# A graph transformer of two layers: layer 1's second weights in seven products too, token sums and shifts moved to GpSimd, the end of each normalization moved to ScalarE

## The chip, the core and the metric

The kernel runs on one core of a Trainium2 chip. The core has five engines, each with an instruction queue of its own that it takes strictly in order: TensorE (PE in the profile), VectorE (DVE), ScalarE (ACT), GpSimd (POOL) and SyncE (SP, which only issues transfers). They wait for each other by semaphores. The metric is the time of the whole program on the device in microseconds, the median over runs.

## The reference

2708 tokens of 512 values go through two layers of the same form. `adj` is a sparse 0/1 matrix, and a token attends only to its neighbours.

```python
q = (h @ Wq.T + bq).reshape(n, 8, 64)      # k, v likewise
scores = where(mask == 0, -1e9, q.k / 8);  attn = softmax(scores)
attn_out = (attn @ v) @ Wo.T + bo
h1 = _layer_norm(h + attn_out, ln1_g, ln1_b)
ff = relu(h1 @ W1.T + b1) @ W2.T + b2      # 512 -> 2048 -> 512
h2 = _layer_norm(h1 + ff, ln2_g, ln2_b)
```

The normalization is `(x - mu) * rsqrt(var + 1e-5) * g + b`. Everything is f32.

## The kernel before, in words

The tokens are sorted by their number of neighbours into 22 groups of 128 (the last has 20), and the groups are taken in 11 blocks of two. Attention goes by lists: for every token GpSimd fetches the key and value rows of its neighbours by gathers (L1113, two neighbours for each of 128 tokens to a chunk). VectorE multiplies and sums them (L1150, L1156, L1182, L1189), and ScalarE takes exponentials and scales the values (L1169, L1176).

The order of all queues is written by hand: each engine gets its instructions in the order in which the Python code records them. For each block the main loop runs over 16 hidden chunks, f = 0 to 15. At each f it records the hidden product on TensorE (`pf`, four products of 128x256) and its relu on ScalarE (`ft`). At some f it records a step of the next block: the `attended` steps at f = 10 to 12 (turned context, output projection `o`, first normalization into `h`), `turned` at f = 15, and as many attention chunks as a table of paces allows (`advance`). So the attention of the next block runs beside the feed-forward of this one.

The feed-forward's second product comes in two forms. In `feed_forward` each hidden chunk meets its half of W2 in two products of 512 columns. In `feed_forward_by_seven`, used in layer 0 for blocks 2 to 9, two hidden chunks and two halves of tokens and of columns are seen as 2x2 matrices, and multiplied by seven products of 128x256 in place of eight, in Winograd's manner. Three more matrices made of W2 (`form`) are fetched for every pair of chunks from `form_d`; four sums of the hidden chunks (`sums`, 128x128 each) are made for each of seven pairs; the eighth pair goes the ordinary way. The results lie in four banks of PSUM, `a0`, `a1`, `c0`, `c1`, and are put together by one copy on ScalarE and eight additions on VectorE. The four banks leave two for hidden products (`ps_f`) where the ordinary form has three.

`norm` (L1265) is the layer normalization: statistics, `mv` and `va` on VectorE, `rd` (a power of -1/2 of one column) on GpSimd, then two passes of VectorE over the 128x512 tile, of which the first subtracts the mean and applies the gain, and the second (L1281) applies `rd` and adds the shift. The shift is `ln1_b + b2` after the first normalization, and `ln2_b` (in layer 0 with the next layer's `bo`) after the second. Since the tile holds more than the product needs, `flip` takes the surplus away while a turned tile is copied out of PSUM (`nb2`, `nbo`, the negated vectors as columns).

In layer 0 the finished `z` tiles are turned and multiplied into the next layer's keys and values during the next block (`keys_values`, f = 5 to 8). In layer 1 they are written to the output by a scatter of GpSimd (`put`).

Of the kernel before, what the change touches and what calls it, by code (L numbers as in the profile page):

```python
# [18 lines left out]
P = 128  # L19
# [35 lines left out]
PACE7 = (0.0,) * 4 + (0.6,) + (1.3,) * 4 + (0.6,) * 2 + (0.0,) * 2 + (0.5, 0.8, 2.4)  # L55
FORMED = 1
FORMS = (3, 5, 7, 9, 11, 13, 15)
# [426 lines left out]
def by_edges(ctx: ExitStack, tc: tile.TileContext, x, xT, adj, layers, out, redo):  # L484
# [71 lines left out]
    form_d = dram.tile([NFC // 2 - 1, 3, P, 2 * P], F32, name="form_d")  # L556
# [81 lines left out]
    def raw_columns(w, names, place):  # L638

        cols = []  # L640
        for i, name in enumerate(names):
# [3 lines left out]
            cols.append((t, raw, 1.0 if name == "bv" else -1.0))  # L645
# [619 lines left out]
    def norm(z, r, gain, shift, st=None, between=None):  # L1265
# [7 lines left out]
        nc.vector.tensor_scalar(va[:r], mv[:r, 1:2], EPS, None, ALU.add)  # L1273
# [7 lines left out]
        nc.vector.scalar_tensor_tensor(z[:r], z[:r], rd[:r], shift[:r], ALU.mult, ALU.add)  # L1281
# [20 lines left out]
    class Layer:  # L1302
# [5 lines left out]
        def load_first(self):  # L1308
# [7 lines left out]
            self.unsettled = raw_columns(w, ("bv", "b2"), place)  # L1316
            self.bv, self.nb2 = [col[0] for col in self.unsettled]
# [15 lines left out]
        def settle(self):  # L1333
            for t in self.unsettled:
                if len(t) == 2:
                    nc.vector.tensor_tensor(t[0], t[0], t[1], ALU.add)
                    continue
                to, raw, sign = t
                pr = ps.tile([P, DM], F32, tag="g", name="pr")
                nc.tensor.transpose(pr[:, :NC], raw, ident[:NC, :NC])  # L1340
                nc.vector.tensor_scalar(to, pr[:, :NC], sign, None, ALU.mult)
            self.unsettled = []
# [20 lines left out]
        def load_next(self):  # L1363
# [4 lines left out]
            self.unsettled += raw_columns(nxt, ("bo",), place)  # L1368
            self.nbo = self.unsettled[-1][0]
# [64 lines left out]
        def attended(self, block, got, xbs=None):  # L1434
# [16 lines left out]
            for i, xb in enumerate(xbs):  # L1451
# [7 lines left out]
                norm(h, r, self.g1, self.e1b2)  # L1459
# [6 lines left out]
        def turned(self, block, hs):  # L1466
            hT = dn.tile([P, NC, 2 * P], F32, tag="hT", name="hT", bufs=1)
            c0 = 0
            for g, h in zip(block, hs):
                r = size(g)  # L1470
                flip(h, r, hT[:, :, c0 : c0 + r], self.nb2)
                c0 += r
            return hT

        def feed_forward(self, block, hs, hT):
# [77 lines left out]
            for g, a, h in zip(block, accs, hs):  # L1553
# [15 lines left out]
                norm(z, r, self.g2, self.e2, st)  # L1569
                if self.n == NL - 1:  # L1570
                    put(out, ident_i[:r, g : g + 1], z[:r], "out")
# [15 lines left out]
        def form(self, j):  # L1587
# [3 lines left out]
            t2, t3, t4 = self.slots if j < NFC // 2 - 2 else self.other_slots  # L1591
# [4 lines left out]
            for i, t in enumerate((t2, t3, t4)):  # L1596
                nc.sync.dma_start(out=form_d[j, i], in_=t)
# [7 lines left out]
        def ask_forms(self, upto):  # L1605

            while self.asked < upto:
                n = self.asked
                j, i = n // 3 % (NFC // 2 - 1), (2, 0, 1)[n % 3]
                nc.sync.dma_start(out=self.slots[i], in_=form_d[j, i])  # L1610
# [471 lines left out]
```

## Time and profile before

| | |
|---|---|
| median of 3 runs | 1830.28 us (1830.05 to 1832.14) |
| span of the profiled execution | 1827.1 us |
| busy: TensorE, VectorE, ScalarE, GpSimd | 1807.5, 1457.5, 949.1, 798.9 us |
| a block of layer 0 in seven products | 75.5 to 76.5 us |
| a block of layer 1 | 63.7 us |

The profile is one execution. A row of time has the start, the length, the engine, the line, the operation, output and inputs, shapes, and in brackets how long the engine was idle before it and what ended that. A row of a group has the count, the busy time, the mean of one in nanoseconds, and the idle time before them. An f32 product appears as two records. Names are those of the program: `kv` a chunk of key and value rows, `pf` a hidden product in PSUM, `ft` and `forms` its relu in SBUF, `h` a tile of the residual stream (also the finished z), `u` the helper tiles of the seven products.

### The profile page before, as it was taken

Reading aid. Unit: us, or ns where it says so; the run is one execution under the profiler, and the core shown is the slowest. Engines: PE = TensorE matmul, PEld = TensorE weight load, DVE = VectorE, ACT = ScalarE, POOL = GpSimd, SP = SyncE. Lnnn points to the kernel's source line nnn. Section 1 sums busy time; section 2 is a strip of 40 time slices with the busy share of each in tenths; the row PEclk is TensorE's granted clock in tenths of the full one; section 3 lists DMA queues with packets and bytes.
Section 4 is the critical chain, followed back from the end, with each engine's and each line's share of the span. In section 5 each row is a group of like instructions: output and inputs, shape, how many; then the busy total and the mean of one; then the engine's idle time right before and its main releaser. Section 6 shows DMA issues by size and latency. Waiting matters only on the chain.

```text
span 1827.1 us, 22528 instructions
## 1 busy us (share of the span) xinstructions
PE 1807.5 (99%) x6563; PEld 1162.6 (64%) x6563; DVE 1457.5 (80%) x2447; ACT 949.1 (52%) x3271; POOL 798.9 (44%) x745
## 2 busy tenths in 40 slices
PE   9999999999999999999999999999999999999998
PEld 4444456666777867778677644666666666666666
DVE  5887778988989889898895257887898888889853
ACT  5771435645556545564543213665665565567531
POOL 3334755534455544454430042353464555456302
PEclk9999999999999999999999999999999999999999
DMA  9997987757576676765652876745564664555300
GB/s 340 369 335 256 371 283 245 236 169 241 195 255 228 197 236 196 219 233 181 228 191 70 287 257 248 285 160 180 178 228 150 228 224 169 195 197 194 133 14 21
DMA packets 158061, 393.80 MB, mean 216 GB/s; under 512 B 17514, under 2 KB 60894, under 8 KB 157928
## 3 DMA queue, kind: packets, MB, share of 16 engines
q0 software_dynamic: 70608, 252.12, 40.2%
q1 hardware_dynamic: 77162, 118.55, 18.7%
q10 hardware_dynamic: 10158, 21.61, 3.1%
q8 instruction: 53, 0.87, 0.2%
q14 instruction: 80, 0.66, 0.1%
HBM read 338.78 MB, written 53.44 MB: 215 GB/s over the span
## 4 chain that ended last, share of the span: by engine, by line
PE 89%; DVE 5%; issue 2%; ACT 2%; DMA 1%; POOL 1%; POOLq 0%; SPq 0%; DVEq 0%
PE pf L1523 18%; PE a L1496 17%; PE pf L1653 9%; PE k L620 8%; PE v L620 8%; PE q L620 8%; PE o L620 8%; PE c L1643 4%; PE a L1643 3%; PE tp L1293 2%; DVE sc L1156 1%; DVE kv L1150 1%; DMA forms<-form_d 1%; PE a L1677 1%; PE a L1673 1%
## 5 line engine op out<-in xcount | busy, mean ns | idle before, releaser
L1113 POOL DMA_INDIRECT kv<-kv_d,listed x420 | 524.0, 1248 | 291.2 <-DVE acc L1189 133.9
L1523 PE MATMUL pf<-hT,w 128*128 128x256 f32 (+1 forms) x1792 | 393.2, 367 | 0.1
L1523 PEld LDWEIGHTS pf<-hT,w 128*128 128x128 f32 x1792 | 323.5, 190 | 103.1 <-issue 64.4
L1496 PE MATMUL a<-w,ft 128*128 128x512 f32 x800 | 373.1, 592 | 0.0
L1176 ACT ACTIVATE kv<-kv,p 128x64 f32<-128x64 f32 x1232 | 311.0, 335 | 5.0
L1275 POOL TENSOR_TENSOR rd<-va,mhalf 128x1 f32<-128x1 f32 (+1 forms) x88 | 80.5, 914 | 520.6 <-DVE va L1273 520.5
L1150 DVE TENSOR_TENSOR kv<-kv,q 128x1024 f32<-128x1024 f32 (+1 forms) x222 | 256.9, 1157 | 13.3 <-DMA q<-q_d,ident_i 10.9
L1156 DVE TENSOR_REDUCE sc<-kv 128x16 f32<-128x1024 f32 (+1 forms) x222 | 257.9, 1162 | 7.6
L1189 DVE TENSOR_TENSOR acc<-acc,kv 128x1024 f32<-128x1024 f32 (+2 forms) x178 | 205.4, 1154 | 37.6 <-ACT kv L1176 23.0
L1653 PE MATMUL pf<-hT,w 128*128 128x256 f32 x1024 | 233.1, 379 | 1.6 <-ACT ft L1664 1.6
L1496 PEld LDWEIGHTS a<-w,ft 128*128 128x128 f32 x800 | 150.1, 190 | 113.2 <-issue 101.3
L1653 PEld LDWEIGHTS pf<-hT,w 128*128 128x128 f32 x1024 | 193.9, 190 | 35.4 <-issue 7.9
L1534 ACT ACTIVATE ft<-pf,b 128x256 f32<-128x256 f32 (+1 forms) x208 | 95.0, 459 | 197.6 <-PE pf L1523 195.2
L1169 ACT ACTIVATE p<-sc,listed 128x8 f32<-128x8 f32 x420 | 104.0, 296 | 147.2 <-DVE sc L1156 135.7
L620 PE MATMUL o<-wo,cT 128*128 128x512 f32 x336 | 151.0, 593 | 1.0 <-ACT cT L1298 1.0
L1664 ACT ACTIVATE ft<-pf,b 128x256 f32<-128x256 f32 x96 | 44.9, 468 | 160.5 <-PE pf L1653 160.5
L1182 DVE TENSOR_TENSOR kv<-kv,p 128x512 f32<-128x512 f32 (+1 forms) x178 | 123.4, 693 | 4.5 <-ACT p L1169 4.3
L620 PEld LDWEIGHTS o<-wo,cT 128*128 128x128 f32 x336 | 63.4, 190 | 74.7 <-issue 65.5
L745 DVE MAX8 tops<-code 128x8 f32<-128x247 f32 (+2 forms) x242 | 78.6, 400 | 28.3 <-ACT code L740 28.3
L1281 DVE SCALAR_TENSOR_TENSOR h<-h,rd,ln_b 128x512 f32<-128x512 f32 (+1 forms) x88 | 65.9, 749 | 39.5 <-POOL rd L1275 39.5
L1220 ACT ACTIVATE cx<-acc,su 128x64 f32<-128x64 f32 (+1 forms) x352 | 88.2, 333 | 12.9 <-DVE su L1212 7.4
L1455 DVE TENSOR_TENSOR h<-o,xb 128x512 f32<-128x512 f32 (+1 forms) x44 | 30.3, 688 | 80.0 <-PE o L620 65.0
(232 smaller groups left out, 2323.5 us busy)
## 6 DMA issues: line engine op xcount, KB each, us to landing
aj<-in_adj SPq DMA_DIRECT2D x42, 677.0 KB, 6.3
forms<-form_d SPq DMA_DIRECT2D x168, 128.0 KB, 4.2
kv_d<-kvs ACTq DMA_DIRECT2D x21, 512.0 KB, 5.5
xg<-in_xT SPq DMA_DIRECT2D x19, 512.0 KB, 7.4
w<-in_W SPq DMA_DIRECT2D x16, 512.0 KB, 6.2
kv<-kv_d,listed POOLq DMA_INDIRECT x420, 6.3
zT_d<-zT SPq DMA_DIRECT2D x22, 256.0 KB, 5.1
xb_d<-h SPq DMA_DIRECT2D x21, 256.0 KB, 5.7
```

Source lines behind the costliest of these rows:

```text
L620: nc.tensor.matmul(o[:r], xs(c), wm[:, c, :], start=(c == 0), stop=(c == NC - 1))
L1113: return nc.gpsimd.indirect_dma_start(out=to, out_offset=None, in_=table[:, :], in_offset=bass.IndirectOffsetOnAxis(ap=s, axis=0), bounds_ ...
L1150: nc.vector.tensor_tensor(kv[:r, :c, :DM], kv[:r, :c, :DM], self.q[:r].unsqueeze(1).to_broadcast([r, c, DM]), ALU.mult,)
L1156: nc.vector.tensor_reduce(self.sc[:r, s0 : s0 + c, :], kv[:r, :c, :DM].rearrange("p s (h d) -> p s h d", d=DK), AX.X, ALU.add,)
L1169: nc.scalar.activation(p[:r, s, :], self.sc[:r, s, :], AF.Exp, bias=minus[:r, g, s : s + 1])
L1176: nc.scalar.activation(to[:, i, hd], kv[:r, i, DM + h * DK : DM + (h + 1) * DK], AF.Copy, scale=p[:r, s0 + i, h : h + 1],)
L1182: nc.vector.tensor_tensor(to[:, 0, :].rearrange("p (h d) -> p h d", d=DK), kv[:r, 0, DM:].rearrange("p (h d) -> p h d", d=DK), p[:r, s0, : ...
L1189: nc.vector.tensor_tensor(self.acc[:r, :c, :], self.acc[:r, :c, :], kv[:r, :c, DM:], ALU.add)
L1496: nc.tensor.matmul(a[:r, cols], fts[f][:, c0 : c0 + r], self.w2[f // 2][:, f % 2, cols], start=(f == 0), stop=(f == NFC - 1),)
L1523: nc.tensor.matmul(pf[:, :w], self.w1[f // 2][:, c, f % 2 * P : f % 2 * P + P], hT[:, c, :w], start=(c == 0), stop=(c == NC - 1),)
L1643: nc.tensor.matmul(to, left, right, start=start, stop=stop)
L1653: nc.tensor.matmul(pf[:, :W], self.w1[j][:, c, f % 2 * P : f % 2 * P + P], hT[:, c, :], start=(c == 0), stop=(c == NC - 1),)
```

## The change

Layer 1 takes the seven products in blocks 0 to 9 (`FIRST7`), with a pace table and a `form_d` of its own. Its three extra matrices are formed in the last block of layer 0 and during the first queries of layer 1, in three places of the gathers' ring (`staged`). All four late query projections of layer 1 are done ahead of its first block, since the place of Wq then holds the fetched forms.

The token sums go from VectorE to GpSimd. In `norm`, `va` goes to GpSimd, and the second pass becomes a scaling on ScalarE without a shift; the shift is added by GpSimd (`shifted`) when the tile has been turned, or, in layer 1, before it is scattered. The columns that `flip` applies now add `ln1_b`, `ln2_b`. Only the two groups of the very last block keep the old second pass.

```diff
+FIRST7 = (FORMED + 1, 0)
...
-    def norm(z, r, gain, shift, st=None, between=None):
+    def norm(z, r, gain, st=None, between=None, shift=None):
...
-        nc.vector.tensor_scalar(va[:r], mv[:r, 1:2], EPS, None, ALU.add)
+        nc.gpsimd.tensor_scalar(va[:r], mv[:r, 1:2], EPS, None, ALU.add)
         rd = small.tile([P, 1], F32, tag="rd", name="rd")
         nc.gpsimd.tensor_tensor(rd[:r], va[:r], mhalf[:r], ALU.pow)
...
         if between:
             between()
-        nc.vector.scalar_tensor_tensor(z[:r], z[:r], rd[:r], shift[:r], ALU.mult, ALU.add)
+        if shift is not None:
+            nc.vector.scalar_tensor_tensor(z[:r], z[:r], rd[:r], shift[:r], ALU.mult, ALU.add)
+            return
+        nc.scalar.activation(z[:r], z[:r], AF.Copy, scale=rd[:r])
+
+    def shifted(z, r, shift):
+        nc.gpsimd.tensor_tensor(z[:r], z[:r], shift[:r], ALU.add)
...
-                norm(h, r, self.g1, self.e1b2)
+                norm(h, r, self.g1)
...
-                flip(h, r, hT[:, :, c0 : c0 + r], self.nb2)
+                flip(h, r, hT[:, :, c0 : c0 + r], self.e1)
                 c0 += r
+            for g, h in zip(block, hs):
+                shifted(h, size(g), self.e1b2)
...
-                norm(z, r, self.g2, self.e2, st)
+                norm(z, r, self.g2, st, shift=self.e2 if apart else None)
...
+        def staged(self):
+
+            slots = []
+            for _ in range(3):
+                place = at.tile([P, SLOTS, 2 * DM], F32, tag="kv", name="forms", bufs=KVB)
...
-                nc.vector.tensor_tensor(s[:, 0], f1[:, P:], f0[:, P:], ALU.add)
...
+                nc.gpsimd.tensor_tensor(s[:, 0], f1[:, P:], f0[:, P:], ALU.add)
+                nc.gpsimd.tensor_tensor(f0[:, P:], f0[:, :P], f0[:, P:], ALU.subtract)
+                nc.gpsimd.tensor_tensor(s[:, 1], s[:, 0], f0[:, :P], ALU.subtract)
+                nc.gpsimd.tensor_tensor(s[:, 2], f1[:, :P], s[:, 1], ALU.subtract)
...
-            norm(zA, P, self.g2, self.e2, between=lambda: stB.append(spread(zB)))
-            norm(zB, P, self.g2, self.e2, stB[0])
+            norm(zA, P, self.g2, between=lambda: stB.append(spread(zB)))
+            norm(zB, P, self.g2, stB[0])
+            if self.n == NL - 1:
+                for g, z in zip(block, hs):
+                    shifted(z, P, self.e2)
+                    put(out, ident_i[:, g : g + 1], z, "out")
...
-                flip(z, r, zT[:, :, :r], self.nbo)
+                flip(z, r, zT[:, :, :r], self.e2c)
                 zTs.append(zT)
+                shifted(z, r, self.e2)
...
-            seven = n == 0 and FORMED < k < NB - 1
+            seven = FIRST7[n] <= k < NB - 1
...
+                    if f > 6 and f % 2:
+                        nxt.form((f - 7) // 2, staged[(f - 7) // 2])
```

How the queues change is seen in three places. The first is ScalarE's queue at the end of a seven block of layer 0; `u` is the copy that begins the putting together, L1664 the next block's relus. Before:

```order
L1176 ACTIVATE acc<-kv,p 128x64 x8
L1695 COPY u_5593<-c_4991 128x256
L1664 ACTIVATE ft<-pf,b_1157 128x256 x4
L1664 ACTIVATE forms<-pf,b_1157 128x256
L1169 ACTIVATE p<-sc,listed 128x8 x2
```

With the change (L1686 are the relus, L1288 the new scaling):

```order
L1180 ACTIVATE acc<-kv,p 128x64 x8
L1717 COPY u_5618<-c_5012 128x256
L1288 ACTIVATE h<-h,rd 128x512 x2
L1686 ACTIVATE ft<-pf,b_1158 128x256 x4
L1686 ACTIVATE forms<-pf,b_1158 128x256
L1173 ACTIVATE p<-sc,listed 128x8 x2
```

Two scalings that read `rd` now stand between the copy of `u` and the next block's relus.

The second is ScalarE's queue around the output projections, f = 10 to 15 of the same block; `cT` is the turned context that a projection reads. Before:

```order
L1298 ACTIVATE cT<-tp,bv 128x128 x4
L1169 ACTIVATE p<-sc,listed 128x8 x2
L1176 ACTIVATE kv<-kv,p 128x64 x8
L1664 ACTIVATE forms<-pf,b_1157 128x256
L1298 ACTIVATE cT<-tp,bv 128x128 x4
L1664 ACTIVATE ft<-pf,b_1157 128x256 x3
```

With the change:

```order
L1308 ACTIVATE cT<-tp,bv 128x128 x4
L1173 ACTIVATE p<-sc,listed 128x8 x2
L1180 ACTIVATE kv<-kv,p 128x64 x8
L1686 ACTIVATE forms<-pf,b_1158 128x256
L1288 ACTIVATE h<-h,rd 128x512
L1308 ACTIVATE cT<-tp,bv 128x128 x4
L1686 ACTIVATE ft<-pf,b_1158 128x256
L1288 ACTIVATE h<-h,rd 128x512
L1686 ACTIVATE ft<-pf,b_1158 128x256 x2
```

The first scaling stands ahead of the second `cT`, the second ahead of the relu of f = 13.

The third is GpSimd's queue at the end of a block of layer 1. Before:

```order
L1275 TENSOR_TENSOR rd<-va,mhalf 128x1
L1076 DMA out<-h,ident_i 2708x512
L1275 TENSOR_TENSOR rd<-va,mhalf 128x1
L1076 DMA out<-h,ident_i 2708x512
L1113 DMA kv<-kv_d_112,listed 128x1024 x14
```

With the change (L1277 is `va`, L1291 a shift, L1647 to L1650 the sums of one pair):

```order
L1277 TENSOR_SCALAR va<-mv 128x1
L1279 TENSOR_TENSOR rd<-va,mhalf 128x1
L1291 TENSOR_TENSOR h<-h,ln_b 128x512
L1080 DMA out<-h,ident_i 2708x512
L1291 TENSOR_TENSOR h<-h,ln_b 128x512
L1080 DMA out<-h,ident_i 2708x512
L1647 TENSOR_TENSOR forms<-ft 128x128
L1648 TENSOR_TENSOR ft<-ft 128x128
L1649 TENSOR_TENSOR forms<-forms,ft 128x128
L1650 TENSOR_TENSOR forms<-ft,forms 128x128
```

Shifts and the next block's sums stand in the queue that held gathers and scatters, and the sums come behind both scatters.

More of the change, by code (lines that the diff above doesn't have):

```diff
@@ L555, in by_edges @@
     xb_d = [None] + [dram.tile([N, DM], F32, name=f"xb_d{n}") for n in range(1, NL)]
-    form_d = dram.tile([NFC // 2 - 1, 3, P, 2 * P], F32, name="form_d")
+    form_d = [dram.tile([NFC // 2 - 1, 3, P, 2 * P], F32, name=f"form_d{n}") for n in range(NL)]
     rec_d = dram.tile([P * NT, 2 * LIST], F32, name="rec_d")
@@ L1912, in by_edges @@
                 next(early[n])
-            streamed = now.queries(order[18 : 2 * AHEAD])
+            streamed = now.queries(order[18:])
             next(streamed)
             now.query(order[17], both[:, 1])
-            advance(0.6)
-            next(streamed)
-            advance(0.6)
+            for _ in order[18:21]:
+                advance(0.6)
+                next(streamed)
             *_, hs = early[n]
             early[n] = hs, now.turned(blocks[0], hs)
-            asking = now.queries(blocks[AHEAD])
-            next(asking)
             finish(streamed)
@@ L1925, in by_edges @@
             now.load_w2(NFC // 2 - 1)
+            now.prepared()
         hs, hT = early[n]
@@ L1960, in by_edges @@
                 if more and f == NFC - 1:
-                    finish(asking)
                     hT = now.turned(blocks[k + 1], hs_next)
-                advance((PACE7 if seven else (PACE if k else PACES)[n])[f])
-                if f in (0, 3, 7, 9) and (f or k):
-                    next(asking, None)
+                advance((PACE7[n] if seven else (PACE if k else PACES)[n])[f])
                 if k == 0 and len(now.w1) < NFC // 2 and f % 2 == 0:
```

52 lines of the change are left out of this document (27 added, 25 removed).

## The prediction

> **What bounds the kernel now.** I read the page first, then the stretches, then the order of time at the ends of blocks.
>
> ```profile
> PE 1807.5 (99%) x6563; PEld 1162.6 (64%) x6563; DVE 1457.5 (80%) x2447; ACT 949.1 (52%) x3271; POOL 798.9 (44%) x745
> ```
>
> Stretches (columns: length, then busy PE, PEld, DVE, ACT, POOL with counts, clock, DMA share, GB/s): one block of layer 0 in seven products, the turn to layer 1, one block of layer 1.
>
> ```profile
> 592.36:668.86 76.50, 75.71 (x311) 56.79 (x311) 67.44 (x114) 43.05 (x164) 37.74 (x30) 1.00 0.67 218
> 1003.00:1058.00 55.00, 54.36 (x251) 31.80 (x250) 16.15 (x33) 9.63 (x27) 4.78 (x5) 1.00 0.82 275
> 1403.40:1467.10 63.70, 63.70 (x226) 41.11 (x225) 55.20 (x72) 39.59 (x149) 33.27 (x28) 1.00 0.56 207
> ```
>
> TensorE sets the time: it has no gap in layer 1 and 0.79 us of gaps in 76.5 in layer 0. So work taken from the others is worth nothing, work taken from TensorE is worth its full time, and any wait put in front of TensorE costs its full time.
>
> **Fewer products.** Two stretches of the chain of waits (start, length, records):
>
> ```profile
> 547.15 10.36 PE pf L1653 x48
> 1398.27 5.15 PE a L1496 x12
> ```
>
> A product is two records. One 512 columns wide takes 2 x 5.15/12 = 0.858 us, one 256 wide 2 x 10.36/48 = 0.432. A layer 1 block had 32 wide ones in its second product: 27.5 us. In seven it has 49 narrow ones (21.2), and for the last pair 2 wide and 4 narrow (3.4): 24.6. The gain is 2.9 us in each of 10 blocks: **-28.8 us**.
>
> **The closing pass on ScalarE.** This step decides. ScalarE now ends each normalization, and takes its queue in order. Its rows at the end of a seven block read: copy u, scale zA, scale zB, then the relus of the next block. The scale of zB needs rd of zB, which needs statistics over the whole finished block. The next block's first hidden product needs no z, but its relu now stands behind that scale. Seven blocks have two places for hidden products, so the third waits for the first one's relu. This is how such a wait looks today, once for 0.79 us:
>
> ```profile
> 666.87 1.99 PE L1653 MATMUL pf<-hT,w 128*128 128x256 f32 x8 [0.79 <-ACT ft L1664]
> ```
>
> The end of a layer 0 block, in order of time:
>
> ```profile
> 622.38 0.59 PE L1643 MATMUL a<-w,forms 128*128 128x256 f32 x2
> 622.81 10.52 PE L1653 MATMUL pf<-hT,w 128*128 128x256 f32 x48
> 624.12 0.37 DVE L1696 TENSOR_TENSOR h<-u,h 128x256 f32<-128x256 f32 x1
> 624.74 0.47 ACT L1664 ACTIVATE ft<-pf,b 128x256 f32<-128x256 f32 x1 [2.65 <-PE pf L1653]
> 628.20 0.68 DVE L1269 BATCH_NORM_STATS2 st<-h 128x6 f32<-128x512 f32 x1
> 629.44 0.93 POOL L1275 TENSOR_TENSOR rd<-va,mhalf 128x1 f32<-128x1 f32 x1 [6.20 <-DVE va L1273]
> 630.46 0.73 DVE L1281 SCALAR_TENSOR_TENSOR h<-h,rd,ln_b 128x512 f32<-128x512 f32 x1
> 631.62 0.93 POOL L1275 TENSOR_TENSOR rd<-va,mhalf 128x1 f32<-128x1 f32 x1 [1.25 <-DVE va L1273]
> ```
>
> The next block starts at 622.81; its first relu follows at 624.74, at once. rd of zB ends at 632.55, 9.7 us after the start. VectorE came late to this chain: its first addition starts 1.3 us after the block's end. The same place with VectorE idle before:
>
> ```profile
> 1003.27 0.42 DVE L1696 TENSOR_TENSOR h<-u,h 128x256 f32<-128x256 f32 x1 [12.19 <-ACT u L1695]
> 1003.91 4.19 PE L1523 MATMUL pf<-hT,w 128*128 128x148 f32 x32
> 1009.67 0.73 DVE L1281 SCALAR_TENSOR_TENSOR h<-h,rd,ln_b 128x512 f32<-128x512 f32 x1
> 1010.83 0.92 POOL L1275 TENSOR_TENSOR rd<-va,mhalf 128x1 f32<-128x1 f32 x1 [1.27 <-DVE va L1273]
> ```
>
> Here rd of zB ends at 1011.75, 7.8 us after the start. In the changed kernel zA's closing pass is gone from between (0.7 us less), and va moves to GpSimd for about what it took on VectorE. That leaves 7.2 to 9.1 us. Then come the scale (nearest row: a ScalarE copy of that shape) and the first relu:
>
> ```profile
> L1737 ACT COPY kvs<-v 128x512 f32<-128x512 f32 x21 | 12.3, 586 | 106.0 <-PE v L620 106.0
> L1664 ACT ACTIVATE ft<-pf,b 128x256 f32<-128x256 f32 x96 | 44.9, 468 | 160.5 <-PE pf L1653 160.5
> ```
>
> So the first relu ends 8.2 to 10.1 us after the block's start, while TensorE wants the third product's place after two (2 x 1.73 = 3.45 us). It stands still for 4.8 to 6.7 us. I take 6.0, nearer the late row, since most blocks are crowded like it. Nothing can cover it: only hidden products stand there in TensorE's queue. Eight blocks of layer 0 and ten of layer 1 end so: 18 x 6.0 = **+108 us** (86 to 121). Late next: everything tied to the next hidden products.
>
> **The same pass in the middle of a block.** The scale of the first h tile now stands ahead of the copy-out of the second cT, which the second o product needs.
>
> ```profile
> 592.19 3.60 PE L620 MATMUL o<-wo,cT 128*128 128x512 f32 x8
> 596.26 1.14 ACT L1298 ACTIVATE cT<-tp,bv 128x128 f32<-128x128 f32 x4 [1.11 <-PE tp L1293]
> 597.97 0.68 DVE L1455 TENSOR_TENSOR h<-o,xb 128x512 f32<-128x512 f32 x1
> 600.66 0.93 POOL L1275 TENSOR_TENSOR rd<-va,mhalf 128x1 f32<-128x1 f32 x1 [0.42 <-DVE va L1273]
> 600.82 3.60 PE L620 MATMUL o<-wo,cT 128*128 128x512 f32 x8
> ```
>
> With these times rd ends at 601.59, the scale at 602.2, the copy-out at 603.3, and the second o starts 2.5 us late. But VectorE took up the first o 2.3 us after it ended; without that lateness the loss is 0.2. The token sums that leave VectorE give part of it back. I take 1.2 in the eight blocks of layer 0, where a bias is added too, and nothing in layer 1: **+10 us** (0 to 20, or 45 if layer 1 pays too).
>
> **Sums and shifts on GpSimd.** 28 sums of 128x128 and four shifts of 128x512 a block; nearest rows: GpSimd's integer sum of 128x128 and its 128x512 sum below.
>
> ```profile
> L734 POOL TENSOR_TENSOR aj<-aj,diag 128x128 int32<-128x128 int32 x20 | 8.7, 433 | 29.6 <-DMA aj<-in_adj 29.6
> 148.07 0.17 DVE L803 TENSOR_TENSOR run<-run 128x22 f32<-128x22 f32 x1
> 148.28 1.29 POOL L958 TENSOR_TENSOR kvs<-kvs,bk 128x512 f32<-128x512 f32 x1 [2.43 <-issue]
> 148.36 1.25 DVE L803 TENSOR_TENSOR run<-run 128x20 f32<-128x20 f32 x1
> ```
>
> That is 28 x 0.43 + 4 x 1.29 = 17.3 us of GpSimd a block. The last row matters: a VectorE sum of two SBUF tiles, 0.17 us by itself, took 1.25 and ended with the GpSimd sum beside it. The two exclude each other. VectorE loses the sums and four closing passes a block, and gets these waits instead. While TensorE pauses 6 us a block, I count both moves as nothing (layer 1's own adds for the seven products too); if GpSimd becomes the bound it is rival 1. The Trainium skill, "SBUF — State Buffer", section "Who interferes with whom", says the same: a VectorE instruction with two SBUF inputs and a GpSimd instruction that reads SBUF block each other for the whole instruction. The trace agrees (1.25 for 0.17).
>
> **TensorE's clock after a pause.** The only long pause in the trace is the program's end:
>
> ```profile
> 1818.00:1819.00 1.00, 0.24 (x2) 0.00 (x0) 0.69 (x2) 0.00 (x0) 0.00 (x0) 1.00 0.09 16
> 1823.00:1824.00 1.00, 0.00 (x0) 0.00 (x0) 0.00 (x0) 0.00 (x0) 0.00 (x0) 0.79 0.62 238
> 1824.00:1825.00 1.00, 0.00 (x0) 0.00 (x0) 0.00 (x0) 0.00 (x0) 0.00 (x0) 0.50 0.13 41
> ```
>
> The last product ends at 1818.24, and the granted clock falls to half at about 1823.6, 5.3 us later. My pauses of 4.8 to 6.7 us lie on both sides of that. How long half speed lasts shows at the program's start:
>
> ```profile
> 1.59 3.36 PE L540 MATMUL pr<-ones 128*128 128x128 f32 x14 [1.59 <-POOL ones L537]
> 612.45 1.04 PE L1293 MATMUL tp<-ident,h 128*128 128x128 f32 x8
> ```
>
> The warm-up products took 0.24 us each for 3.4 us, later ones of that size 0.13 or less. If a pause costs as much, 1.7 us is lost; with half of 18 pauses affected: **+15 us** (0 to 31). The Trainium skill, "TensorE: Matmul & The Clock Gate", Part 1, puts the gate on free-running windows of about 3.4 us; by it nearly every pause of 6 us would cost this, and the term would be near its upper end.
>
> **The turn between layers.** Forming layer 1's second weights is 28 subtractions:
>
> ```profile
> L1595 DVE TENSOR_TENSOR forms<-w,forms 128x256 f32<-128x256 f32 x7 | 3.0, 425 | 0.2
> ```
>
> That is 12 us on VectorE, which is busy 16 of 55 us there. But it waits in order for weights that have just been loaded, and the SP queue's loads and z tiles stand behind 21 writes of forms. I take **+2 us** (0 to 12, all of it on the path).
>
> **Sum.** 1827.1 - 28.8 + 108 + 10 + 15 + 2 = 1933.3 us of span. The median before lies 3.2 us above the profiled span (1830.28), so 1936.5.
>
> **Rivals.**
> 1. GpSimd becomes the bound in layer 1.
>
> ```profile
> L1113 POOL DMA_INDIRECT kv<-kv_d,listed x22 | 26.6, 1209 | 6.6 <-issue 5.7 <-ACT ft L1534 0.6 <-DVE sc L1156 0.3
> L1150 DVE TENSOR_TENSOR kv<-kv,q 128x1024 f32<-128x1024 f32 x10 | 12.2, 1216 | 0.0
> L1189 DVE TENSOR_TENSOR acc<-acc,kv 128x1024 f32<-128x1024 f32 x8 | 9.8, 1225 | 0.8
> L1182 DVE TENSOR_TENSOR kv<-kv,p 128x512 f32<-128x512 f32 x9 | 6.2, 685 | 0.0
> ```
>
> In the block from 1403.4 it has 33.3 us of work and 6.6 of issue gaps; with 17.3 more (va not counted) 57. VectorE holds two-input operations 28 us of 63.7 by these rows (44%), so each of 36 added ones waits about 0.27 us: 10 more. With some 3 us idle until the end chain is ready (an estimate) that is 70 us, against the 66.8 that I forecast for a block (63.7 - 2.9 + 6.0). 10 x 3.2 on top: about 1970. For it: the sums stand behind gathers in one queue. Against: pauses give it time. Chance 0.17.
> 2. The pauses are long and every one halves the clock, and layer 1 pays at the second o too: 121 + 45 + 31 in place of 108 + 10 + 15: about 2000. Chance 0.11.
> 3. Faster: the relus do not stand behind the scales in effect, because the chain is done before TensorE needs the place. Then the full 28.8 us come out: about 1801. It decides from 1.6 us a pause (28.8/18): the chain would have to end within 4.0 us of the block's end (3.45 + 1.6 less scale and relu), where the earliest row has 7.8. For it: VectorE is relieved. Against: the eight additions and the statistics alone go from 1003.27 past 1008. Chance 0.06.
> 4. The change does not do what it says, pauses and gain cancel: 1830. Chance 0.02.
>
> **How the numbers follow.** The forecast has 0.64. Predicted: 1936 us. Its low end is pauses of 4.8 us and no other loss: 1827.1 - 28.8 + 86 + 3.2 = 1888; its high end takes all upper bounds (121, 20, 31, 12): 1986. The range 1885 to 1995 takes that in, with rival 1 and a part of rival 2; about 2 in 10 lie outside. Slower by over 0.2% (what a measurement here can tell from nothing) is 0.64 + 0.17 + 0.11 = 0.92, within 0.02, faster 0.06.
>
> **What would show it.** Right: at each of 18 block ends TensorE idle 5 to 7 us ahead of the third hidden product, released by a relu, and ScalarE idle ahead of the second scale, released by rd; layer 1 blocks of 66 to 68 us, layer 0 of 82 to 84. Clock below 1.00 behind the pauses if the clock term holds. Rival 1: TensorE waits for GpSimd's sums at the seven products. Wrong: layer 1 blocks near 61 us, or first relus that come before the scales.

## The result, and the profile after

The changed kernel takes 2127.1 us (median of four runs, 2123.2 to 2128.5) against 1831.2 for the kernel before beside it: 1.162 times, interval 1.160 to 1.163. The prediction had the sign, but 1936 us and a range up to 1995. The profiled execution has a span of 2126.5 us.

The page's row of busy time, and from its view of slices the TensorE clock:

```profile
PE 1860.7 (87%) x7023; PEld 1286.4 (60%) x7023; DVE 1422.9 (67%) x2137; ACT 997.1 (47%) x3367; POOL 1252.2 (59%) x1423
...
PEclk9999999898999999999999999898989989999898
```

TensorE was busy 99% of the span and is busy 87%. It has fewer products to do (28.8 us less by the prediction's prices), yet is busy 53 us more: some of its time runs at a lower clock (0.96 and 0.91 in the two blocks below, 1.00 in those of the prediction). What it waited for, from the view of waits (us in total, times, longest):

```profile
PE pf L1675 <- ACT ft L1686: 168.0, 21, 12.6
PE o L624 <- ACT cT L1308: 58.9, 22, 5.8
PE pf L1534 <- ACT ft L1545: 10.5, 2, 5.4
...
PE c L1665 <- POOL forms L1649: 0.5, 1, 0.5
```

The first row is the wait that the prediction named: a hidden product, its place, a relu. Sixteen of the 18 block ends named there are in it, with one more and four short waits; the other two, of 5.4 us each, are in rows of L1534, where the next block has the ordinary form. Together the 18 pauses are 163 us. The last row is rival 1's sign, a wait for GpSimd's sums; it comes once. One block of layer 0 and one of layer 1, as stretches (columns as in the prediction):

```profile
686.60:774.70 88.10, 77.72 (x312) 57.71 (x311) 59.07 (x73) 44.71 (x164) 58.36 (x67) 0.96 0.57 187
1450.40:1529.60 79.20, 64.44 (x271) 51.04 (x270) 59.16 (x75) 42.22 (x157) 58.52 (x65) 0.91 0.61 199
```

76.5 has become 88.1 where 82 to 84 was predicted (88 to 95 in all blocks of that kind), and 63.7 has become 79.2 where 66 to 68 was (72 to 83 in all). Layer 1 is the farthest off, so one of its block ends is shown in order of time. Rows of four engines, picked by their place in the chain; TensorE begins a block at 1686.92:

```profile
1681.82 2.50 POOL L1291 TENSOR_TENSOR h<-h,ln_b 128x512 f32<-128x512 f32 x2
...
1682.08 3.34 DVE L1154 TENSOR_TENSOR kv<-kv,q 128x1024 f32<-128x1024 f32 x1
...
1686.92 3.62 PE L1675 MATMUL pf<-hT,w 128*128 128x256 f32 x16
...
1692.89 0.42 DVE L1718 TENSOR_TENSOR h<-u,h 128x256 f32<-128x256 f32 x1
...
1698.01 0.78 POOL L1277 TENSOR_SCALAR va<-mv 128x1 f32<-128x1 f32 x1 [7.19 <-DVE mv L1275]
...
1700.47 1.41 POOL L1279 TENSOR_TENSOR rd<-va,mhalf 128x1 f32<-128x1 f32 x1
...
1701.91 0.72 ACT L1288 ACTIVATE h<-h,rd 128x512 f32<-128x512 f32 x1 [1.71 <-POOL rd L1279]
...
1703.05 4.33 PE L1675 MATMUL pf<-hT,w 128*128 128x256 f32 x12 [12.51 <-ACT ft L1686]
```

The chain is the predicted one: va, rd, scale of zB, relu, third hidden product. It starts late. VectorE's first addition comes 6.0 us after the block's start; the late row before had 1.3. At 1682.08 a multiplication that takes 1.22 us alone takes 3.34, with two shifts of GpSimd beside it; behind it VectorE has attention's work to do, without a gap, until the addition. So rd of zB ends 15.0 us after the start in place of 7.2 to 9.1, and the pause is 12.5. Seven of the nine such block ends of layer 1 have the addition 4.2 to 6.6 us late, two 0.4; in layer 0 it is 1.1 to 1.9 at six of seven. From the first addition to the end of rd of zB it takes 8.9 to 9.0 us at 14 of these 16 ends and 8.4 at two. In the kernel before it took 8.4 to 8.5, and the prediction had 7.7.

### The profile page after: what moved, and what is told of

It is laid out like the page before. It is cut to its first block, busy times and chain, and to the rows that moved or that the text cites. A ratio compares the mean times of both kernels' runs of the same rounds, so it can differ in the third digit from the quotient of the medians.

```text
span 2126.5 us, 24687 instructions
## 1 busy us (share of the span) xinstructions
PE 1860.7 (87%) x7023; PEld 1286.4 (60%) x7023; DVE 1422.9 (67%) x2137; ACT 997.1 (47%) x3367; POOL 1252.2 (59%) x1423
## 5 line engine op out<-in xcount | busy, mean ns | idle before, releaser
L1675 PE MATMUL pf<-hT,w 128*128 128x256 f32 x2304 | 563.4, 399 | 168.9 <-ACT ft L1686 168.0
L1675 PEld LDWEIGHTS pf<-hT,w 128*128 128x128 f32 x2304 | 460.4, 201 | 257.2 <-ACT ft L1686 176.3
L1288 ACT ACTIVATE h<-h,rd 128x512 f32<-128x512 f32 (+1 forms) x86 | 62.1, 722 | 542.4 <-POOL rd L1279 533.7
L1277 POOL TENSOR_SCALAR va<-mv 128x1 f32<-128x1 f32 (+1 forms) x88 | 62.7, 713 | 366.4 <-DVE mv L1275 366.1
L624 PE MATMUL o<-wo,cT 128*128 128x512 f32 x336 | 176.3, 675 | 59.2 <-ACT cT L1308 58.9
L1686 ACT ACTIVATE ft<-pf,b 128x256 f32<-128x256 f32 x216 | 97.6, 462 | 121.8 <-PE pf L1675 117.9
L1291 POOL TENSOR_TENSOR h<-h,ln_b 128x512 f32<-128x512 f32 (+1 forms) x86 | 120.7, 1418 | 27.5 <-PE tp L1303 26.7
L1534 PE MATMUL pf<-hT,w 128*128 128x256 f32 (+1 forms) x512 | 101.2, 348 | 16.4 <-ACT ft L1545 10.5
L1534 PEld LDWEIGHTS pf<-hT,w 128*128 128x128 f32 x512 | 85.8, 199 | 41.5 <-issue 16.7
L1647 POOL TENSOR_TENSOR forms<-ft 128x128 f32<-128x128 f32 x90 | 51.7, 574 | 81.5 <-ACT ft L1686 62.5
L1665 PE MATMUL a<-w,forms 128*128 128x256 f32 x324 | 96.4, 379 | 0.0
L1665 PE MATMUL c<-w,forms 128*128 128x256 f32 x324 | 96.4, 379 | 0.0
```

The source lines that it names most:

```text
L624: nc.tensor.matmul(o[:r], xs(c), wm[:, c, :], start=(c == 0), stop=(c == NC - 1))
L1291: nc.gpsimd.tensor_tensor(z[:r], z[:r], shift[:r], ALU.add)
L1534: nc.tensor.matmul(pf[:, :w], self.w1[f // 2][:, c, f % 2 * P : f % 2 * P + P], hT[:, c, :w], start=(c == 0), stop=(c == NC - 1),)
L1665: nc.tensor.matmul(to, left, right, start=start, stop=stop)
L1675: nc.tensor.matmul(pf[:, :W], self.w1[j][:, c, f % 2 * P : f % 2 * P + P], hT[:, c, :], start=(c == 0), stop=(c == NC - 1),)
```

## The experiments

All times are medians; a ratio is to the kernel before on the same chip, with its 95% interval. Line numbers shift a little between kernels. Two ladders are built: the change undone piece by piece, and the seven products alone.

**The scaling off ScalarE, or later on ScalarE.** In the first kernel one line of the change is undone:

```diff
-        nc.scalar.activation(z[:r], z[:r], AF.Copy, scale=rd[:r])
+        nc.vector.tensor_scalar(z[:r], z[:r], rd[:r], None, ALU.mult)
```

> One line of the changed kernel: the closing pass of the normalization (a scaling by rd) goes from ScalarE back to VectorE; va, the token sums and the shifts stay on GpSimd, layer 1 stays in seven products. Theory (ScalarE's queue order makes the loss): no relu and no copy of a turned context stands behind a scaling any more, so the waits of hidden products for relus (168.0 + 10.5 us in the changed kernel), most of those of o for cT (58.9 us) and the slow clock behind them (about 82 us) go: 2127 - 178 - 59 - 82 = 1808, with VectorE's 40 more passes 1800 to 1840. Rival (GpSimd's queue, or VectorE and GpSimd excluding each other, sets the block): the time stays above 1950.

In the second the work stays on ScalarE, recorded later:

```diff
+        late.append(lambda: nc.scalar.activation(z[:r], z[:r], AF.Copy, scale=rd[:r]))
...
+                if f in (4, 13, 14):
+                    flush()
```

> The scalings stay on ScalarE, but are recorded later: those of a block's end after the relu of f = 4 of the next block, those of the first normalization after the relus of f = 13 and 14; layer 1's last shift and scatter move with them. Same work on the same engines, only another place in ScalarE's queue. Theory (queue order): 1800 to 1850, and the hidden products no longer wait for relus at block ends. Rival (the engines chosen, the exclusion of VectorE and GpSimd): above 1950, with the same idle time elsewhere.

Measured: 1973.2 us (1.079, 1.077 to 1.082) and 1959.9 us (1.072, 1.070 to 1.075). The waits of the kernel with the closing pass on VectorE:

```profile
PE c L1665 <- POOL forms L1649: 96.2, 17, 12.3
PE tp L1303 <- DVE h L1288: 14.7, 10, 4.0
PE o L624 <- ACT cT L1308: 12.6, 6, 5.6
PE pf L1675 <- ACT ft L1686: 6.0, 5, 1.9
```

The pauses for relus go (168.0 to 6.0), those of `o` mostly (58.9 to 12.6). So the queue position did make them, and the same work later in the same queue is as good. But the times stay 133 and 110 us above the theory's upper ends, where the rivals' numbers were. Layer 0 is nearly healed (blocks of 76 to 83 us); layer 1 is not (mostly 71 to 80): the 0.5 us of waiting for GpSimd's sums is now 96. It had been hidden, because a TensorE that stands still at the block's start comes late to the sums too. The kernel with later scalings shows, in order of time, how the sums come late (VectorE's first addition, GpSimd, TensorE; the block begins at 1624.0):

```profile
1627.97 0.42 DVE L1729 TENSOR_TENSOR h<-u,h 128x256 f32<-128x256 f32 x1
...
1633.09 0.78 POOL L1283 TENSOR_SCALAR va<-mv 128x1 f32<-128x1 f32 x1 [7.19 <-DVE mv L1281]
...
1635.56 1.40 POOL L1285 TENSOR_TENSOR rd<-va,mhalf 128x1 f32<-128x1 f32 x1
...
1636.93 0.44 POOL L1656 TENSOR_TENSOR forms<-ft 128x128 f32<-128x128 f32 x1
...
1638.38 0.70 PE L1674 MATMUL c<-forms 128*128 128x256 f32 x2 [3.38 <-POOL forms L1658]
```

Now it is GpSimd that stands at the head of a queue: 7.19 us idle for the statistics of a VectorE that is late, with the next block's first sums behind. So each theory held half: ScalarE's queue is worth about 151 us (1.162 less 1.079, of 1829), and something else holds layer 1.

**The pauses filled.** Idle products that keep TensorE busy while it would wait:

```diff
+                if f == 1 and k > FIRST7[self.n]:
+                    kept_warm(self)
```

> The changed kernel with 8 (layer 0) or 10 (layer 1) idle products of 128x512 on TensorE, whose result nobody reads, behind the hidden product of f = 1 of every seven block but the first of each layer. They lie in the pause at the block's end (6.4 to 12.6 us), and take nothing away from what waits. Theory (half speed behind a pause is a loss of its own): the products after these pauses run at full speed; of about 82 us of slow clock some 17 pauses' share, 30 to 55 us, comes back: 2070 to 2100; the waits for relus at f = 2 shrink to what the added products don't cover. Rival (the clock costs nothing beyond the pause): 2127 or a little more.

Measured: 2108.1 us (1.153, 1.152 to 1.155), less gain than either bound of the theory, but a gain with 146 products more. TensorE's busy time is 1963.7 us; less the 146 products (125.3 us at 0.858 each, 127.9 by their own row) that is 1836 to 1838, against 1860.7. So 22 to 25 us of slow clock came back over 16 filled pauses, about 1.5 us each. The prediction's price (1.7 us) was near, its count (half of 18) too low. The other 57 to 60 us above 1778.7 (1807.5 less the 28.8 of fewer products) lie elsewhere, for one thing behind the pauses of `o`. How much of it is clock stays open: the kernel below with less attention, which waits little, is 18 us above 1778.7 too (1797.0), and no run shows the 28.8 us in full.

**The normalization's moves alone.** Layer 1 in the ordinary form, sums on VectorE:

```diff
-FIRST7 = (FORMED + 1, 0)
+FIRST7 = (FORMED + 1, 99)
...
-                nc.gpsimd.tensor_tensor(s[:, 0], f1[:, P:], f0[:, P:], ALU.add)
+                nc.vector.tensor_tensor(s[:, 0], f1[:, P:], f0[:, P:], ALU.add)
```

> The changed kernel with layer 1's second product in the ordinary form and the token sums on VectorE: what is left of the change are the normalization's moves (va and shift to GpSimd, the closing pass to ScalarE) and the queries taken ahead. Theory (scalings ahead of relus hold TensorE whatever form the second product has): layer 0's blocks as in the changed kernel, 88 to 92 us, +100 to +130 us; layer 1's blocks lose too, though the ordinary form has a third place for hidden products, 1.7 us less a pause than the 9.2 us there, so 6 to 10 us a block with the clock: 2000 to 2070. Rival (it takes the two places of the seven products): layer 1's blocks stay at 64 to 66 us, 1930 to 1975.

Measured: 2062.2 us (1.127, 1.125 to 1.129), within the theory. Its waits:

```profile
PE pf L1534 <- ACT ft L1545: 73.9, 12, 9.5
PE pf L1675 <- ACT ft L1686: 72.0, 10, 11.8
PE o L624 <- ACT cT L1308: 25.0, 20, 3.9
```

L1534 is the ordinary form: three places for hidden products do not save it, the pauses there are 5.1 to 9.5 us, all but one. The head of ScalarE's queue is the cause, not the number of places.

**The seven products alone.** Three kernels, all with va, sums and closing pass on VectorE. In the first the shift is added by GpSimd as in the change; in the second it is left out; the third is the kernel before with layer 1 in seven products and what that needs (the forming, the queries done ahead, layer 1's pace table), and nothing else of the change.

```diff
     def shifted(z, r, shift):
-        nc.gpsimd.tensor_tensor(z[:r], z[:r], shift[:r], ALU.add)
+        return
```

> The changed kernel with va, the token sums and the closing pass on VectorE as before; what is left of the change is layer 1 in seven products, and the shift added by GpSimd after the turning. Theory (the 28.8 us are there to be had, the moves took them): 1800 to 1815. Rival (VectorE, 55 us busy of a 63.7 us block, can't take sums and the putting together of the seven products in layer 1, which was the use of the moves): 1830 to 1870, with TensorE waiting for sums or for the first normalization.

> The kernel with seven products in layer 1, va, sums and closing pass on VectorE (1961 us), with the shift on GpSimd left out, so that the residual lacks it and the result is not the reference's. Theory (the shifts on GpSimd keep VectorE out and stand ahead of gathers and scatters): 1890 to 1915, and VectorE's multiplications of 128x1024 back from 1.215 to 1.16 us. Rival (the loss comes from the form of the closing pass or the turning): 1940 or more.

> The kernel before with layer 1 in seven products and nothing else of the change: the normalization, its shift and the token sums stay where they were. Theory now (in layer 1 the first sums of a block come late, behind the end of the block before on the same queue, and VectorE comes late to that end): blocks of layer 1 of 70 to 76 us in place of 63.7, TensorE waiting for the first sums and at half speed after it, 1900 to 1960. Rival, the prediction's first step (the fewer products are worth 28.8 us by themselves, the moves took it): 1800 to 1815.

Measured: 1961.1 us (1.072, 1.070 to 1.074), 1902.5 us (1.040, 1.038 to 1.041) and 1911.7 us (1.045, 1.043 to 1.046). For the first both numbers were too low, the rival nearer; the other two went by the theory. The third denies the prediction's first step: fewer products on TensorE, no moves, and the kernel is 81 us slower. The turn between the layers has about 6 us of that: query products there come first 1.1 us later than in the kernel before (1054.61 for 1053.50), then 7.1 (1106.36 for 1099.24). Between them TensorE waits 4.4 us for a tile of VectorE, which has just waited 8.5 us for weights to form. The rest lies in the blocks of layer 1. One of them:

```profile
1593.90:1666.40 72.50, 64.79 (x270) 50.91 (x270) 65.99 (x109) 39.49 (x151) 35.16 (x27) 0.95 0.62 215
```

and three of its waits:

```profile
PE pf L1666 <- ACT ft L1677: 28.9, 17, 3.7
PE c L1656 <- DVE forms L1640: 23.1, 8, 4.7
PE o L624 <- ACT cT L1302: 22.3, 8, 6.4
```

VectorE is busy 66.0 of 72.5 us, where TensorE's products of a block need 60.8 (63.7 - 2.9). In the block before it VectorE's queue has no gap over 0.5 us in the first 37 us. The 28 sums, 0.29 us each here, are 8.0 us; the eight additions that put the results together 4.4; two additions of 0.68 fall away. That makes 11 us on top of the 55.2 that the prediction quoted. The blocks take 62 to 77 us, more than VectorE's work alone: the rest is waits of TensorE as in the three rows, and slow clock (0.95) behind them.

The shift costs 59 us when it is on GpSimd (1902.5 to 1961.1). The two kernels have the same 2815 instructions on VectorE. The page's row of busy time and two groups, first of the kernel with shifts, then without:

```profile
PE 1835.2 (94%) x7023; PEld 1271.2 (65%) x7023; DVE 1620.4 (83%) x2815; ACT 952.4 (49%) x3281; POOL 912.8 (47%) x831
```

```profile
L1154 DVE TENSOR_TENSOR kv<-kv,q 128x1024 f32<-128x1024 f32 (+1 forms) x222 | 269.7, 1215 | 14.7 <-DMA q<-q_d,ident_i 11.5 <-DMA kv<-kv_d,listed 3.0 <-issue 0.2
...
L1649 DVE TENSOR_TENSOR forms<-forms,ft 128x128 f32<-128x128 f32 x90 | 46.4, 516 | 0.0
```

```profile
PE 1811.7 (95%) x7023; PEld 1258.6 (66%) x7023; DVE 1540.1 (81%) x2815; ACT 950.7 (50%) x3281; POOL 794.3 (42%) x745
```

```profile
L1154 DVE TENSOR_TENSOR kv<-kv,q 128x1024 f32<-128x1024 f32 (+1 forms) x222 | 257.2, 1159 | 14.7 <-DMA q<-q_d,ident_i 11.5 <-DMA kv<-kv_d,listed 3.1
...
L1649 DVE TENSOR_TENSOR forms<-forms,ft 128x128 f32<-128x128 f32 x90 | 25.6, 285 | 0.0
```

86 shifts lengthen VectorE's same work by 80.3 us, 0.93 each: about two thirds of the 1.42 us that a shift takes there on the mean are paid again on VectorE. What part of the 59 us comes of that, and what of the shifts' place in GpSimd's queue ahead of gathers and scatters, no run separates.

**Is it VectorE's load?** Two ways of giving it less in layer 1: leaving out part of the attention, and taking seven products only in the two blocks with the least attention beside them.

```diff
-            if s0:
+            if s0 and self.n == 0:
                 nc.vector.tensor_tensor(
                     self.acc[:r, :c, :], self.acc[:r, :c, :], kv[:r, :c, DM:], ALU.add
```

> The kernel with layer 1 in seven products and everything else as before, and the accumulation of the weighed values left out in layer 1 (about nine VectorE additions of 128x1024 a block, 1.22 us each), so the result of layer 1's attention is not the reference's; TensorE's work is the same. Theory (VectorE is full: 64 to 68 us busy in blocks of 68 to 76 us of layer 1, where TensorE needs 60.9): with 11 us less of it the blocks fall to 61 to 64 us, 1825 to 1850 in all. Rival (the order of the queues, not their load): the waits stay, above 1880.

```diff
-FORMED = 1
+FORMED = (1, 7)
...
-            seven = n == 0 and FORMED < k < NB - 1
+            seven = FORMED[n] < k < NB - 1
```

> The kernel before with seven products in blocks 8 and 9 of layer 1 alone, whose three more matrices are formed in block 7 as layer 0 does in its block 1; nothing at the turn of the layers, no moves between engines. These two blocks have the least attention beside them. Theory (where VectorE has time the 2.9 us a block are there): 1823 to 1829, faster by 0 to 0.4%. Rival (forming and putting together cost as much): 1832 to 1845.

Measured: 1843.7 us (1.007, 1.005 to 1.009) for the first, within the theory's time, with blocks a little above its 61 to 64 us. A block of it:

```profile
1547.90:1613.30 65.40, 63.24 (x272) 50.40 (x271) 55.65 (x99) 39.61 (x152) 32.36 (x27) 0.97 0.67 234
```

With VectorE back at 55.7 us, blocks fall from some 72 to some 65. So its load is the main cause. Still all but the last stay above 60.8, and even this kernel, with work missing, only comes near the one before; 10 us of waits for fetched forms, 8 for relus and 7 for turned contexts are left in it, which no run separates further.

The second went against the theory: 1853.8 us (1.014, 1.012 to 1.016), slower than even its rival. Block 7, in which the matrices are formed, and block 9:

```profile
1600.00:1669.00 69.00, 64.71 (x218) 40.44 (x217) 62.91 (x91) 40.22 (x153) 27.38 (x24) 0.95 0.55 198
1738.00:1806.90 68.90, 60.61 (x272) 48.91 (x271) 45.37 (x87) 25.21 (x92) 9.71 (x8) 0.95 0.25 79
```

In the first VectorE is at 63 of 69 us: the 28 subtractions of forming (12 us by the prediction's row) fill it. In the second it has time (45 us), but TensorE once stands 6.83 us for a relu, which is behind the scaling of the last attention's result on ScalarE; by then the attention runs late. The gain of 2 x 2.9 us is less than one such wait.

**The sums on GpSimd.** First alone, in the kernel before (layer 0 only); then in layer 1 only, with the old normalization.

```diff
-                nc.vector.tensor_tensor(s[:, 0], f1[:, P:], f0[:, P:], ALU.add)
+                nc.gpsimd.tensor_tensor(s[:, 0], f1[:, P:], f0[:, P:], ALU.add)
```

> The kernel before with one move: the token sums of layer 0's eight seven blocks on GpSimd. The prediction counted this as nothing: 1826 to 1833. Theory now (VectorE and GpSimd keep each other out, GpSimd's gathers come later): 1 to 2 us a block, 1836 to 1848.

> The kernel with layer 1 in seven products and the old normalization, with the token sums of layer 1 alone on GpSimd. Theory (VectorE's load is the bound of layer 1): 8 us of VectorE a block less and some waits for GpSimd, blocks of 64 to 68 us, 1850 to 1890. Rival (on GpSimd the sums wait behind gathers, rd and scatters as in the kernel with the sums ahead): no better than the 1912 with the sums on VectorE.

Measured: 1833.9 us (1.003, 1.002 to 1.004), between the two; and 1913.6 us (1.047, 1.045 to 1.049), the rival, no gain over 1911.7. The page of the first:

```profile
PE 1809.6 (99%) x6563; PEld 1162.3 (63%) x6563; DVE 1419.2 (77%) x2223; ACT 948.8 (52%) x3271; POOL 937.9 (51%) x969
```

VectorE loses 224 sums of 0.29 us, 65 us of work, but its busy time falls only by 38.3 (from 1457.5): 27 us come back as longer instructions beside GpSimd's sums (its multiplications of 128x1024 take 1.185 us on the mean, 1.157 before). In layer 1 the wait changes its engine. From the second kernel, the first row of its waits, and a row of GpSimd's order of time:

```profile
PE c L1657 <- POOL forms L1641: 57.6, 10, 9.5
```

```profile
1594.11 1.00 POOL L1279 TENSOR_TENSOR rd<-va,mhalf 128x1 f32<-128x1 f32 x1 [8.66 <-DVE va L1277]
```

Again rd, which waits for VectorE, is ahead of the block's first sums in GpSimd's queue. Three kernels take that order away. The first is the one with later scalings, with va and rd recorded behind the first sums; the second also turns layer 0's finished tiles one hidden chunk later; the third does the first with the old normalization, which has no shifts, in layer 1 alone, with the closing passes on VectorE behind rd and the scatters behind the second sums:

```diff
                 if f % 2 == 0 and j > 0:
                     sums(j - 1)
+                if f == 2:
+                    flush(late)
+                if f == 4:
+                    flush(puts)
```

> The kernel with the later scalings, and va and rd of a seven block's end recorded on GpSimd behind the first token sums of the next block (the scalings then behind the relu of f = 5). The work is the same. Theory (GpSimd's order: va and rd, which wait for VectorE's late statistics, stand ahead of the first sums, and TensorE waits for these): the 73.9 us of waits for the sums and the slow clock behind them go, 1957 - 74 - 20 to 35, so 1845 to 1880. Rival (VectorE with 57 to 63 us of work in layer 1's blocks is the bound there, and the wait only moves on): above 1925.

> As the kernel before it, and in seven blocks the finished tiles of layer 0 are turned one hidden chunk later (f = 6 to 9 in place of 5 to 8). Theory: the waits of the turning for the scalings in layer 0 (17.0 us in the kernel with the later scalings, up to 2.1 a block) go: 8 to 20 us less than its neighbour. Rival (they only hide another wait): no difference.

> As the kernel with the old normalization and layer 1's sums on GpSimd (1913.6 us), with rd of a layer 1 block's end recorded on GpSimd behind the first sums of the next block, the closing passes on VectorE behind that, and the scatters of the output behind the second sums. Work and engines are the same. Theory (what is left is GpSimd's order): the 57.6 us of waits for sums and about 20 us of slow clock go, 1835 to 1865. Rival (the wait moves to later sums behind gathers, as it did in the kernel with the sums ahead): 1885 to 1915.

Measured: 1956.8 us (1.070, 1.068 to 1.071), the rival: nothing gained over 1959.9. The wait moved on to the third pair's sums, behind shifts, scatters and gathers (rows in order of time):

```profile
1653.62 1.54 POOL L1309 TENSOR_TENSOR h<-h,ln_b 128x512 f32<-128x512 f32 x1
...
1655.45 1.72 POOL L1080 DMA_INDIRECT out<-h,ident_i  x1 [0.28 <-POOL h L1309]
...
1661.58 1.02 POOL L1117 DMA_INDIRECT kv<-kv_d,listed  x1 [0.30 <-issue]
...
1662.62 0.47 POOL L1668 TENSOR_TENSOR forms<-forms 128x128 f32<-128x128 f32 x1
...
1665.41 2.08 PE L1686 MATMUL c<-forms 128*128 128x256 f32 x4 [7.58 <-POOL forms L1670]
```

The second: 1934.5 us (1.057, 1.055 to 1.058), 22 us less than its neighbour, a little more than expected; the waits of the turning fell from 31.8 to 7.4 us, and 7.6 us of waits for the turned tiles came in their place. The third: 1882.1 us (1.028, 1.027 to 1.030), 31 us less than with the same engines in the other order (of rd, closing passes and scatters together), but short of the theory's 1865. Its waits:

```profile
PE pf L1687 <- ACT ft L1698: 25.7, 16, 4.0
PE o L624 <- ACT cT L1319: 17.5, 6, 5.6
PE c L1677 <- POOL forms L1661: 9.8, 6, 3.9
```

The waits for sums are all but gone (57.6 to 9.8), and relus and turned contexts, the things that come from attention's pace, take a part of their place. No version beats the kernel before: the best one with all ten blocks of layer 1 in seven products that leaves nothing out is this one. One rival stays untested: every kernel with seven products in layer 1 has the change's pace table there, and whether attention recorded at other places would leave VectorE less late, no run shows.

## Why the prediction was wrong

By the ratios, in one order of adding the parts (each of 1829 us):

| step | predicted | measured |
|---|---|---|
| seven products in layer 1, with the turn between layers | -28.8 + 2 | +81 |
| shift on GpSimd, apart from the closing pass | 0 | +51 |
| va and sums on GpSimd | 0 | +13 |
| closing pass on ScalarE: pauses, second `o`, clock | 108 + 10 + 15 | +151 |
| sum | +106 | +296 |

The shares depend on the order: with the ordinary form in layer 1 the normalization's moves alone cost 232 us, and the seven products and the sums on top of them 64, since a TensorE that pauses gives VectorE time. The sum does not depend on it. No kernel of layer 1 in seven products gains, in either order.

**Fewer products** is the step that failed. It said that work taken from TensorE is worth its full time, since TensorE sets the time. That was read from the kernel before, and the same step loads VectorE. Its row stood in the prediction: 55.20 of 63.70 us busy. With 11 us more VectorE needs 66 us where TensorE needs 60.8, so it is VectorE that is full, and TensorE waits for it: +81 us in place of -26.8. Taking VectorE's load back, by leaving out work, took 68 of the 81 us away. The turn between the layers, put at 2 us, has about 6. The prediction dismissed "layer 1's own adds for the seven products too" in a bracket, by the very pauses that it forecast.

**Sums and shifts at nothing** failed for the same reason. The exclusion of the two engines was seen in one row (1.25 for 0.17) and judged to be covered. It is paid where VectorE is full: 0.93 us for each shift. The Trainium skill, "SBUF — State Buffer", section "Who interferes with whom", says that a VectorE instruction with two SBUF inputs contends with a GpSimd instruction that reads SBUF. The pair of runs with and without shifts agrees with it: VectorE's sums of L1649 take 516 and 285 ns. The prediction named the rule and set no price on it.

**The closing pass on ScalarE** was right in place and mechanism: the pauses vanish when the scaling goes to VectorE or later into ScalarE's queue, and come with the ordinary form too. The 133 us are near the 151 only because other waits come out when the pauses go. In the trace of the change the 18 pauses are 163 us, where 108 was forecast and 121 was the upper bound, and the waits of `o` for turned contexts 58.9, where 10 was. Two terms within the pause were mis-sized: "VectorE came late" was taken as 1.3 us from a block of layer 0, which holds there, but in layer 1 it is mostly 4.2 to 6.6; and the chain from the first addition to rd of zB was to lose 0.7 us and gains 0.5. va was put at what it took on VectorE (0.15 us) and takes 0.78, twice; the second rd mostly takes 1.4. The second `o` was put at nothing in layer 1, and waits there too. The wait that the prediction shows as happening once in the kernel before is there twice, 0.8 us each; nothing rests on it.

**The clock** behind a pause: about 1.5 us measured, 1.7 predicted; the half of 18 pauses was wrong, all of them and many of the shorter ones at `o` were followed by slow products.

**The rivals.** Rival 1, GpSimd as the bound, was not the cause of the result (0.5 us of waiting for sums). But it was ready behind it. The rival named the gathers ahead of the sums and counted GpSimd's work; what held the first sums was rd, waiting at the head of the queue for a late VectorE, and how much the load adds behind it no run separates. Rival 2 had the right members (long pauses, clock each, layer 1's `o`), and was still 127 us short: it too had the gain of 28.8 us in it and nothing for sums and shifts, and its pauses were 121 us, not 163.

## What to carry to other kernels

When work is taken from the engine that sets the time, count what the same step adds to the next one, and compare that sum with the shortened stage before counting the gain. Moving work off a full engine onto an in-order queue that also feeds the main one can cost more than it frees: ask what stands behind the moved instruction, and whether its input comes from the late engine. A long wait hides others; after it is removed in an experiment, read the waits again before believing the sum.

## What the runs showed of the hardware

The clock can halve sooner than the prediction took from the program's end (5.3 us). Rows of `o` products behind pauses, of the changed kernel; the same eight records take 3.70 us at full clock:

```profile
1656.20 3.70 PE L624 MATMUL o<-wo,cT 128*128 128x512 f32 x8 [2.62 <-ACT cT L1308]
476.54 5.40 PE L624 MATMUL o<-wo,cT 128*128 128x512 f32 x8 [2.79 <-ACT cT L1308]
1975.97 5.25 PE L624 MATMUL o<-wo,cT 128*128 128x512 f32 x8 [3.03 <-ACT cT L1308]
```

There is no sharp edge: in the kernel with the first sums ahead, a pause of 2.60 us was followed by a slow product,

```profile
1606.12 5.31 PE L624 MATMUL o<-wo,cT 128*128 128x512 f32 x8 [2.60 <-ACT cT L1319]
1675.03 3.70 PE L624 MATMUL o<-wo,cT 128*128 128x512 f32 x8 [2.59 <-ACT cT L1319]
```

and one of 2.59 was not. Over all kernels of this study pauses of 3.1 us and more ahead of a full `o` (eight records as above) were always followed by slow products, those of 2.0 to 3.1 us sometimes. The granted clock in stretches of 1 us shows when it falls: 3.5 us after TensorE's last product in the row at 476.54 above, so 0.7 us into the `o`, and 2.5 us after it in the row at 1606.12. It stays at half for 3.4 us both times. The Trainium skill, "TensorE: Matmul & The Clock Gate", Part 1, states free-running windows of about 3.4 us, and the slow clock after at least one idle one. A scatter and the 3.4 us at half speed fit such windows, but pauses shorter than one whole window already cost half speed here; on this point the measurement decides.

A one-column instruction on GpSimd is not free: `va` takes 0.71 us there on the mean, 0.15 on VectorE (groups of the changed kernel, and of the one before):

```profile
L1277 POOL TENSOR_SCALAR va<-mv 128x1 f32<-128x1 f32 (+1 forms) x88 | 62.7, 713 | 366.4 <-DVE mv L1275 366.1
```

```profile
L1273 DVE TENSOR_SCALAR va<-mv 128x1 f32<-128x1 f32 (+1 forms) x88 | 13.5, 153 | 3.1
```
